# Attention denominators: three of eight weight blocks summed by accumulating transfers into DRAM, one of eight on TensorE, four on VectorE

## The chip, the cores and the metric

The kernel runs on one core of one Trainium2 chip. The metric is device time in microseconds (us). The kernel before takes 4078.07 us, the median of 2 runs (4075.41 to 4080.73).

## The reference, cut to what matters

Two graph layers over 4096 nodes with 512 features in 4 heads, all in float32. Layer 0 runs attention twice (an encoder and a decoder with the same weights), layer 1 once. For every attention the unnormalised weight of source node m for target node n is a masked function of two scalars, and the output row is divided by the sum of its weights.

```python
# layer 0: scores = sigmoid(f1[n] + f2[m]), masked by the adjacency, softmax over m
sig = jax.nn.sigmoid(f1[:, :, None] + f2[:, None, :])
local_att = _masked_softmax(local_pattern[None] * sig, lmask)
Xa = jnp.einsum('hij,hjd->hid', att, Xw)          # encoder
Y = jnp.einsum('hij,hjd->hid', att, Yh)           # decoder, the same att
# layer 1: leaky ReLU of e_s[n] + e_n[m], masked, softmax over m
attn = jax.nn.softmax(logits, axis=-1)
out = jnp.einsum('hnm,hmo->hno', attn, feats)
```

The denominator of the softmax is the sum of the weights over m. How that sum is formed is what the change alters.

## The kernel before, in words

The three attentions are called "enc", "dec" and "gat" and are all built by one function, `attention` (L204). It loops over two blocks of 2048 target nodes (`tb`) and four heads (`h`); one such pass is called a pair here, and each attention has 8 pairs. Inside a pair, `j` (L241) runs over the 32 blocks of 128 source nodes. Block j works on one tile `e` of 128 x 2048 float32 (1024 KB): 128 source nodes on the partitions, 2048 targets along the row.

For each j the weights are computed into `e` and then used:

- enc (and three blocks of four in dec): ScalarE runs a tanh (L288) and an exp (L289) on the whole tile, VectorE multiplies by the 0/1 mask (L290).
- gat: ScalarE runs one Relu (L439), VectorE one fused add-and-multiply (L440).
- TensorE multiplies the tile with the value block of the head, four products of 512 columns, into four PSUM tiles `po` that accumulate over all j (L255).
- In enc, each block with j % 4 = 3 is also stored to DRAM (`ekeep`, L253, from the SP queue); dec loads those again instead of computing them (L249). Masks are loaded from the SP queue for two blocks at a time (L245).

Denominators are formed in enc and gat only (`sums` is set); dec uses the reciprocals of enc again. Before the change, `e` of the blocks with j % 8 in (1, 4, 6) is summed over its partitions by a product with a matrix of ones on TensorE (`add_to_den`, L234 to L237, four products of 32 output rows, into the PSUM tile `den`). The other five of eight are added up on VectorE into a tile `acc` (the first by a copy, L262, the others L265). At the end of a pair `acc` goes through the ones product too; `den` is copied (L275), sent through DRAM in three small transfers from the POOL queue (L277, L279, L282), spread over all partitions as `rb` (L283) and multiplied onto the outputs on GpSimd (L296 in enc, L449 in gat). In gat a Relu (L450), transposes on TensorE (L453) and an addition (L455) follow.

What sets the order of work around the change: the tiles `e` come from a pool of three buffers (`epool`, bufs=3), so ScalarE can begin a tile only when everything that reads the third tile before it is done: the products, the addition or ones product, and any store of it. `po` comes from a pool of seven PSUM banks, `den` from one. Each engine runs its instructions in the order that the scheduler wrote; transfers are issued by SP or POOL in the order of those queues, and a queue that waits holds everything behind it. The rows of scores for a later pair (`rowb`, L224) also go through POOL.

Of the kernel before, what the change touches and what calls it, by code (L numbers as in the profile page):

```python
# [26 lines left out]
FP = mybir.dt.float32  # L27
U8 = mybir.dt.uint8
AF = mybir.ActivationFunctionType
ALU = mybir.AluOpType  # L30
# [4 lines left out]
N, F, H, D, P = 4096, 512, 4, 128, 128  # L35
# [5 lines left out]
TB = 2048  # L41
NTB = N // TB
# [20 lines left out]
def kernel(ctx, tc, x, adjT, w0, w0T, v0, wencT, wdecT, vecs, w1, w1T, a1, out):  # L63
    nc = tc.nc
    consts = ctx.enter_context(tc.tile_pool(name="consts", bufs=1))
    big = ctx.enter_context(tc.tile_pool(name="big", bufs=1))
    dram = ctx.enter_context(tc.tile_pool(name="dram", bufs=1, space=DRAM))
# [34 lines left out]
    rows = [dram.tile([H, IB], FP, name=f"rows{i}") for i in range(NIB)]  # L102
    dens = [[dram.tile([SB, IB], FP, name=f"dens{h}_{t}") for t in range(NTB)] for h in range(H)]
    rinvs = [[dram.tile([1, TB], FP, name=f"rinvs{h}_{t}") for t in range(NTB)] for h in range(H)]

    ekeep = [[[dram.tile([P, TB], FP, name=f"ekeep{h}_{t}_{k}") for k in range(NJ // 4)] for t in range(NTB)]
             for h in range(H)]
# [6 lines left out]
    def everywhere(d, row=0):  # L114

        n = d.shape[-1]
        return bass.AP(tensor=d.tensor, offset=d.offset + row * n, ap=[[0, P], [1, n]])
# [86 lines left out]
    def attention(what, weights, finish, rowprep=None, evacuate=None, sums=None, kept=None):  # L204

        with tc.tile_pool(name=f"{what}_a", bufs=2 if evacuate else 3) as apool, tc.tile_pool(name=f"{what}_r", bufs=2) as rpool, \
                tc.tile_pool(name=f"{what}_e", bufs=3) as epool, tc.tile_pool(name=f"{what}_s", bufs=1) as spool, \
                tc.tile_pool(name=f"{what}_po", bufs=7, space=PSUM) as po_pool, \
                tc.tile_pool(name=f"{what}_ps", bufs=1, space=PSUM) as ps_pool:
            for tb in range(NTB):  # L220
                for h in range(H):
                    rowb = rpool.tile([P, TB], FP, name="rowb")
                    for s in range(SB):
                        nc.gpsimd.dma_start(rowb[:, s * IB:(s + 1) * IB], everywhere(rows[tb * SB + s], h))  # L224
                    if rowprep is not None:
                        rowprep(rowb, h)
                    rb = spool.tile([P, TB], FP, name="rb")
                    if sums is None:
                        nc.gpsimd.dma_start(rb, everywhere(rinvs[h][tb]))
                    else:  # L230
                        acc = spool.tile([P, TB], FP, name="acc")
                        den = ps_pool.tile([P, IB], FP, name="den")

                    def add_to_den(t, start, stop):  # L234
                        for s in range(SB):
                            nc.tensor.matmul(den[s * 32:(s + 1) * 32, :], ones, t[:, s * IB:(s + 1) * IB],  # L236
                                             start=start, stop=stop)  # L237

                    po = [po_pool.tile([P, IB], FP, name="po") for _ in range(SB)]
                    first = True  # L240
                    for j in range(NJ):  # L241
                        e = epool.tile([P, TB], FP, name="e")
                        if j % AG == 0:
                            a2 = apool.tile([P, AG, TB], U8, name="a2")
                            nc.sync.dma_start(a2, masks[tb][j // MG][(j % MG) * P:(j % MG + AG) * P, :]  # L245
                                              .rearrange("(t p) i -> p t i", p=P))
                        store = j % 4 == 3 and kept is not None
                        if store and kept == "read":
                            nc.sync.dma_start(e, ekeep[h][tb][j // 4])  # L249
                        else:  # L250
                            weights(e, rowb, a2[:, j % AG, :], j, h)
                            if store:
                                nc.sync.dma_start(ekeep[h][tb][j // 4], e)  # L253
                        for s in range(SB):
                            nc.tensor.matmul(po[s], V[j // C][:, j % C, h * D:(h + 1) * D], e[:, s * IB:(s + 1) * IB],  # L255
                                             start=(j == 0), stop=(j == NJ - 1))
                        if sums is None:
                            continue
                        if j % 8 in (1, 4, 6):
                            add_to_den(e, j == 1, False)  # L260
                        elif first:
                            nc.vector.tensor_copy(acc, e)  # L262
                            first = False
                        else:
                            nc.vector.tensor_add(acc, acc, e)  # L265
                    if evacuate is None:
                        outs = [X[tb * SB + s][:, h, :] for s in range(SB)]
                        for s in range(SB):
                            nc.scalar.copy(outs[s], po[s])  # L269
                    else:  # L270
                        outs = evacuate(spool, h, po)
                    if sums is not None:
                        add_to_den(acc, False, True)
                        dsb = spool.tile([P, IB], FP, name="dsb")
                        nc.scalar.copy(dsb, den)  # L275

                        nc.gpsimd.dma_start(dens[h][tb], dsb[0:P:32, :])  # L277
                        dcol = spool.tile([P, TB // P], FP, name="dcol")
                        nc.gpsimd.dma_start(dcol, dens[h][tb].rearrange("s (q k) -> (s q) k", k=TB // P))  # L279
                        nc.vector.tensor_scalar(dcol, dcol, sums[0], None, sums[1])  # L280
                        nc.vector.reciprocal(dcol, dcol)  # L281
                        nc.gpsimd.dma_start(rinvs[h][tb].rearrange("o (p k) -> (o p) k", k=TB // P), dcol)  # L282
                        nc.gpsimd.dma_start(rb, everywhere(rinvs[h][tb]))  # L283
                    for s in range(SB):
                        finish(h, tb * SB + s, outs[s], rb[:, s * IB:(s + 1) * IB], spool, po_pool)
# [12 lines left out]


    attention("enc", tanh_weights, finish_enc, sums=(TINY, ALU.max), kept="write")  # L300


# [43 lines left out]
    def finish_dec(h, ib, xs, rb, spool, po_pool):  # L346
# [5 lines left out]
        nc.vector.scalar_tensor_tensor(xs, xs, 0.0, ex, ALU.max, ALU.add)  # L352

    attention("dec", tanh_weights, finish_dec, kept="read")


# [91 lines left out]
    def finish_gat(h, ib, o, rb, spool, po_pool):  # L448
# [7 lines left out]
        if h == H - 1:  # L456
            nc.sync.dma_start(out[ib * IB:(ib + 1) * IB, :].rearrange("(c p) f -> p c f", p=P), X[ib])

    attention("gat", gat_weights, finish_gat, rowprep_gat, evac_gat, sums=(N * TINY, ALU.add))


# [39 lines left out]
```

## Time and profile before

| | |
|---|---|
| median of 2 runs | 4078.07 us |
| profiled execution, its own time | 4079.67 us |
| span of that execution | 4077.9 us |
| granted TensorE clock, mean over the span | 0.951 |
| PE / DVE / ACT / POOL busy | 3588.5 / 2812.2 / 2531.6 / 228.4 us |
| HBM read / written | 407.53 / 92.67 MB |

The span is the time from the first to the last instruction of one profiled execution. PE is TensorE's matmuls, PEld its weight loads, DVE is VectorE, ACT is ScalarE, POOL is GpSimd; "SPq" and "POOLq" in a line is a transfer being issued there. In the list of groups a line reads: source line, engine, operation, output<-inputs, shapes, count | busy us, mean ns of one instruction | idle time of the engine just before those instructions and what ended it. A float32 product of 512 columns is two matmul instructions in the trace, so one `add_to_den` shows as 8. In a timeline the columns are start in us, duration in us, engine, line, operation, count, and in brackets the idle time before it and its releaser. The line numbers are those of the kernel before; the change shifts those below it by two to thirteen.

### The profile page before, as it was taken

The page shows a single profiled execution, that of the slowest core. Times are in us where ns is not written, and L with a number is a line of the kernel's source. Part 1 is how long each engine was busy: PE and PEld are TensorE (multiplying, and loading weights), DVE is VectorE, ACT ScalarE, POOL GpSimd, SP SyncE. Part 2 cuts the span into 40 slices and gives each one's busy share as a digit, 9 for nine tenths or more (in the row PEclk, how much of TensorE's full clock was granted, in tenths as well). Part 3 has the DMA queues.
Part 4 walks back from the last instruction along what each step waited for, and adds up shares of the span by engine and source line. Part 5 has one row for each costly group of instructions (what it writes and reads, how often), then busy time and mean ns, then how long its engine had stood idle before and what let it go on. Part 6 is the DMA issues. An engine that isn't in the chain of part 4 may idle for free. (4 is left out here: it accounts for less than half of the span.)

```text
span 4077.9 us, 27394 instructions
## 1 busy us (share of the span) xinstructions
PE 3588.5 (88%) x10312; PEld 1554.0 (38%) x10312; DVE 2812.2 (69%) x1965; ACT 2531.6 (62%) x1607; POOL 228.4 (6%) x280
## 2 busy tenths in 40 slices
PE   0979999999999789999999999799879889988987
PEld 0733333333333354333334344355333333333432
DVE  2468888898889654555454556832779779778876
ACT  0178988998889248777778874211445445445543
POOL 0000000000000000000000000000000000000000
PEclk9989999999999899999999999889889889989988
DMA  9834434443433124344443442200222122222112
GB/s 166 88 119 145 135 134 138 136 141 128 144 129 119 42 57 146 143 165 158 151 160 141 153 154 78 77 7 1 79 71 78 62 73 78 104 73 83 62 62 88
DMA packets 159253, 434.89 MB, mean 107 GB/s; under 512 B 12176, under 2 KB 12688, under 8 KB 139536
## 3 DMA queue, kind: packets, MB, share of 16 engines
q1 hardware_dynamic: 137408, 365.07, 25.4%
q0 software_dynamic: 20992, 67.51, 8.6%
q8 instruction: 81, 1.33, 0.1%
q10 hardware_dynamic: 720, 0.55, 0.0%
q14 instruction: 52, 0.43, 0.0%
HBM read 407.53 MB, written 92.67 MB: 123 GB/s over the span
## 5 line engine op out<-in xcount | busy, mean ns | idle before, releaser
L255 PE MATMUL po<-e,V 128*128 128x512 f32 x6144 | 2770.2, 606 | 155.1 <-DVE e L290 113.4
L255 PEld LDWEIGHTS po<-e,V 128*128 128x128 f32 x6144 | 1157.3, 193 | 1765.4 <-issue 1481.6
L290 DVE TENSOR_TENSOR e<-e,a 128x2048 f32<-128x2048 f32 x448 | 1023.9, 2289 | 569.6 <-ACT e L289 565.6
L288 ACT ACTIVATE e<-rowb,jcol 128x2048 f32<-128x2048 f32 x448 | 893.0, 1995 | 259.6 <-PE po L255 176.7
L289 ACT ACTIVATE e<-e 128x2048 f32<-128x2048 f32 x448 | 854.1, 1910 | 12.7
L439 ACT ACTIVATE e<-rowb,nq,jcol 128x2048 f32<-128x2048 f32 x256 | 535.9, 2094 | 463.5 <-PE po L255 255.7
L265 DVE TENSOR_TENSOR acc<-acc,e 128x2048 f32<-128x2048 f32 x304 | 696.6, 2291 | 10.0
L440 DVE SCALAR_TENSOR_TENSOR e<-e,jcol,a 128x2048 f32<-128x2048 f32 x256 | 599.5, 2347 | 76.7 <-ACT e L439 73.4
L236 PE MATMUL den<-e,ones 128*32 128x512 f32 x1536 | 207.8, 613 | 18.6 <-DVE e L440 13.9
L224 POOL DMA_DIRECT2D rowb<-rows x96 | 51.9, 548 | 2380.0 <-ACT e L288 1332.2
L406 PE MATMUL pv<-w1s,hT 128*128 128x512 f32 x256 | 139.8, 638 | 1.8 <-ACT hT L145 1.8
L453 PE MATMUL po<-ident,og 128*128 128x128 f32 x128 | 35.7, 434 | 120.1 <-ACT og L450 117.3
L308 ACT ACTIVATE re<-z,vec 128x512 f32<-128x512 f32 x64 | 44.0, 688 | 146.8 <-DVE ex L307 146.8
L321 PE MATMUL z<-X,wenc 128*128 128x512 f32 x256 | 111.6, 599 | 22.6 <-DVE X L163 22.6
L144 PE MATMUL pt<-ident,hn 128*128 128x128 f32 x256 | 37.4, 295 | 93.8 <-DVE hn L141 93.8
L321 PE MATMUL z<-X,wdec 128*128 128x512 f32 x256 | 110.1, 592 | 3.1 <-ACT X L269 3.1
L145 ACT ACTIVATE hT<-pt 128x512 f32<-128x512 f32 x64 | 35.2, 595 | 118.5 <-PE pt L144 118.5
L450 ACT ACTIVATE og<-og,vec 128x512 f32<-128x512 f32 x32 | 23.1, 722 | 125.1 <-POOL og L449 125.1
L121 ACT ACTIVATE rstd<-rstd 128x32 f32<-128x32 f32 x2 | 0.5, 229 | 156.4 <-DVE rstd L120 156.4
L236 PEld LDWEIGHTS den<-e,ones 128*32 128x32 f32 x1536 | 30.4, 108 | 165.1 <-issue 140.3
L455 DVE TENSOR_TENSOR X<-X,po 128x512 f32<-128x512 f32 x32 | 22.0, 688 | 102.6 <-PE po L453 102.6
L408 ACT COPY V<-pv 128x512 f32<-128x512 f32 x32 | 18.8, 586 | 112.4 <-PE pv L406 112.4
(117 smaller groups left out, 1511.7 us busy)
## 6 DMA issues: line engine op xcount, KB each, us to landing
a<-mask SPq DMA_DIRECT2D x384, 512.0 KB
ekeep<-e SPq DMA_DIRECT2D x64, 1024.0 KB
e<-ekeep SPq DMA_DIRECT2D x64, 1024.0 KB
rowb<-rows POOLq DMA_DIRECT2D x96, 256.0 KB, 6.7
rb<-rinvs POOLq DMA_DIRECT2D x24, 1024.0 KB, 5.3
mask<-in_adjT POOLq DMA_DIRECT2D x8, 2048.0 KB, 111.8
X<-in_x SPq DMA_DIRECT2D x8, 1024.0 KB
xt<-in_x SPq DMA_DIRECT2D x8, 1024.0 KB
```

What stands on the lines that cost most here:

```text
L224: nc.gpsimd.dma_start(rowb[:, s * IB:(s + 1) * IB], everywhere(rows[tb * SB + s], h))
L236: nc.tensor.matmul(den[s * 32:(s + 1) * 32, :], ones, t[:, s * IB:(s + 1) * IB], start=start, stop=stop)
L255: nc.tensor.matmul(po[s], V[j // C][:, j % C, h * D:(h + 1) * D], e[:, s * IB:(s + 1) * IB], start=(j == 0), stop=(j == NJ - 1))
L265: nc.vector.tensor_add(acc, acc, e)
L288: nc.scalar.activation(e, rowb, AF.Tanh, bias=jcol[:, j, h:h + 1], scale=0.5)
L289: nc.scalar.activation(e, e, AF.Exp, scale=0.5)
L290: nc.vector.tensor_mul(e, e, a)
L308: nc.scalar.activation(re, src, AF.Relu, bias=bias)
L321: nc.tensor.matmul(z, w[:, fb, o * P:(o + 1) * P], X[ib][:, fb, :], start=(fb == 0), stop=(fb == C - 1))
L406: nc.tensor.matmul(pv, lhsT, w1s[:, fb, :], start=(fb == 0), stop=(fb == C - 1))
L439: nc.scalar.activation(e, rowb, AF.Relu, bias=nq[:, j, h:h + 1], scale=jcol[:, j, h:h + 1])
L440: nc.vector.scalar_tensor_tensor(e, e, jcol2[:, j, h:h + 1], a, ALU.add, ALU.mult)
```

## The change

The split of the denominator sum over the 32 blocks of a pair is new in enc and gat; dec is untouched. Blocks with j % 8 = 3 (four of a pair) go through the ones product on TensorE. Blocks with j % 8 in (1, 4, 6) (twelve of a pair) are sent from `e` to DRAM by transfers from the POOL queue: the first two are plain writes into the two tiles `dacc` of the pair, the other ten add to them in the transfer, alternating between the two. Blocks with j % 8 in (0, 2, 5, 7) (sixteen of a pair, one copy and fifteen additions) are added up on VectorE. At the end of the pair both `dacc` tiles are loaded through the SP queue into tiles of the same pool of three, and each goes through the ones product, ahead of `acc`.

```diff
--- before.py
+++ after.py
@@ -102,6 +102,8 @@
     rows = [dram.tile([H, IB], FP, name=f"rows{i}") for i in range(NIB)]
     dens = [[dram.tile([SB, IB], FP, name=f"dens{h}_{t}") for t in range(NTB)] for h in range(H)]
     rinvs = [[dram.tile([1, TB], FP, name=f"rinvs{h}_{t}") for t in range(NTB)] for h in range(H)]
+
+    dacc = [[[dram.tile([P, TB], FP, name=f"dacc{h}_{t}_{k}") for k in range(2)] for t in range(NTB)] for h in range(H)]
 
     ekeep = [[[dram.tile([P, TB], FP, name=f"ekeep{h}_{t}_{k}") for k in range(NJ // 4)] for t in range(NTB)]
              for h in range(H)]
@@ -237,7 +239,7 @@
                                              start=start, stop=stop)
 
                     po = [po_pool.tile([P, IB], FP, name="po") for _ in range(SB)]
-                    first = True
+                    first, moved = True, []
                     for j in range(NJ):
                         e = epool.tile([P, TB], FP, name="e")
                         if j % AG == 0:
@@ -256,8 +258,15 @@
                                              start=(j == 0), stop=(j == NJ - 1))
                         if sums is None:
                             continue
-                        if j % 8 in (1, 4, 6):
-                            add_to_den(e, j == 1, False)
+                        if j % 8 == 3:
+                            add_to_den(e, j == 3, False)
+                        elif j % 8 in (1, 4, 6):
+                            d = dacc[h][tb][len(moved) % 2]
+                            if len(moved) < 2:
+                                nc.gpsimd.dma_start(d, e)
+                            else:
+                                nc.gpsimd.dma_start(d, e, accum_op=ALU.add)
+                            moved.append(j)
                         elif first:
                             nc.vector.tensor_copy(acc, e)
                             first = False
@@ -270,6 +279,10 @@
                     else:
                         outs = evacuate(spool, h, po)
                     if sums is not None:
+                        for d in dacc[h][tb]:
+                            e = epool.tile([P, TB], FP, name="e")
+                            nc.sync.dma_start(e, d)
+                            add_to_den(e, False, False)
                         add_to_den(acc, False, True)
                         dsb = spool.tile([P, IB], FP, name="dsb")
                         nc.scalar.copy(dsb, den)
```

## The prediction

> **What bounds the kernel now.** I read the groups first: which engine has most work, and what each piece costs.
>
> ```profile
> L255 PE MATMUL po<-e,V 128*128 128x512 f32 x6144 | 2770.2, 606 | 155.1 <-DVE e L290 113.4
> L290 DVE TENSOR_TENSOR e<-e,a 128x2048 f32<-128x2048 f32 x448 | 1023.9, 2289 | 569.6 <-ACT e L289 565.6
> L288 ACT ACTIVATE e<-rowb,jcol 128x2048 f32<-128x2048 f32 x448 | 893.0, 1995 | 259.6 <-PE po L255 176.7
> L289 ACT ACTIVATE e<-e 128x2048 f32<-128x2048 f32 x448 | 854.1, 1910 | 12.7
> L439 ACT ACTIVATE e<-rowb,nq,jcol 128x2048 f32<-128x2048 f32 x256 | 535.9, 2094 | 463.5 <-PE po L255 255.7
> L265 DVE TENSOR_TENSOR acc<-acc,e 128x2048 f32<-128x2048 f32 x304 | 696.6, 2291 | 10.0
> L236 PE MATMUL den<-e,ones 128*32 128x512 f32 x1536 | 207.8, 613 | 18.6 <-DVE e L440 13.9
> ```
>
> The ones products are cheap: 1536 instructions are 192 blocks, 207.8 / 192 = 1.08 us each (four products of 32 rows overlap), against 2770.2 / 768 = 3.6 us for the main products of one block. Next, the table of windows, cut by pair, from one issue of L277 to the next. Columns: busy us with counts for PE, PEld, DVE, ACT, POOL, then clock, DMA share, GB/s. First a pair of enc, then of gat:
>
> ```profile
> core 0: us, PE busy (x) PEld busy (x) DVE busy (x) ACT busy (x) POOL busy (x), PEclk, DMA share, GB/s
> 644.88:782.88 138.00, 129.51 (x361) 49.96 (x360) 119.10 (x59) 125.16 (x70) 9.88 (x12) 0.98 0.41 137
> 3311.93:3459.51 147.58, 130.12 (x376) 52.94 (x376) 122.14 (x59) 74.37 (x43) 9.92 (x13) 0.93 0.23 72
> ```
>
> Enc is paced by ScalarE: 125 of 138 us busy, 3.85 us a block in the timeline, where the ready weights then hold TensorE and VectorE. Gat is paced by TensorE: 3.5 us a block plus 1.05 for each ones product, 8 x 3.5 + 3 x 1.05 = 31.2 us per eight blocks, and some 20 us at the pair's end. Dec has no sums.
>
> Then the three buffers of `e`. The timeline of a stored block in enc shows how much time a transfer that reads `e` has:
>
> ```profile
> 418.88 0.33 SPq L253 DMA_DIRECT2D ekeep<-e  x1
> ...
> 423.85 2.00 ACT L288 ACTIVATE e<-rowb,jcol 128x2048 f32<-128x2048 f32 x1 [0.35 <-DMA ekeep<-e]
> ```
>
> The store starts as the mask product ends, lands in 4.97 us, and ScalarE has already waited 0.35 us for it. There is no spare time: whatever holds a tile longer than about 5.3 us stalls ScalarE. What transfers cost (queue 1 of the page, then issues, the last number us to landing):
>
> ```profile
> q1 hardware_dynamic: 137408, 365.07, 25.4%
> rb<-rinvs POOLq DMA_DIRECT2D x24, 1024.0 KB, 5.3
> ```
>
> A POOL transfer of 1024 KB takes 5.3 us from issue to landing. Queue 1 moves 365.07 MB in 25.4% of 4077.9 us, 2.84 us per MB, so one more pass of 1024 KB (1.05 MB) costs the 16 engines 3.0 us.
>
> **What the skill says.** "DMA: Bandwidth & Descriptors", section "Rules for kernel authors", says that an accumulating transfer reads its destination and writes it later, so that the next one on the same bytes must wait for its semaphore; the built instruction order has these waits on POOL. "Collectives: The Full Stack", section "The bandwidth ceiling: the fold count and why AG ≠ RS ≠ AR", says the add itself is free but needs two source reads, so a reduction runs at about half the rate of a copy. No row of this trace has an accumulating transfer, so this is the unknown. "SBUF — State Buffer", section "Who interferes with whom", says a VectorE operation with two SBUF inputs contends with GpSimd reads; the L277 issues take 0.59 us in enc and up to 1.45 in gat, which would fit.
>
> **The change, part by part**, per pair.
>
> Removed and moved on TensorE: before 12 + 1 ones products, now 4 + 2 + 1, so 6 x 1.05 = 6.3 us less. In gat that is on the pacing engine. In enc it is hidden behind ScalarE, except for its waits on ones products: 22.6 us in 880 us (6.4 pairs), 3.5 us a pair, which I credit. VectorE loses 4 of 20 operations, 4 x 2.29 = 9.2 us, hidden: it has 119 of 138 and 122 of 148 us. If it were the bound this would be a gain; it is not.
>
> Added: 2 plain writes, 10 accumulating transfers, 2 loads. Call T the time of an accumulating transfer from issue to landing. A plain one is 5.3 (the `rb` row). With a second read, 5.3 + 3.0 = 8.3 on idle engines. Only the added 3.0 has not been measured beside other traffic; at a DMA share of 0.41 in enc it becomes 3.0 / 0.59 = 5.1, at about 0.2 in gat 3.0 / 0.8 = 3.7. So T = 10.4 in enc and 9.0 in gat. Bounds: 5.3 (the read fully overlapped) and about 16 (three times the added pass and more).
>
> Enc, stalls. ScalarE's start on block j+3 waits for the transfer of j: 3.85 (tanh, exp) + 0.05 + 2.29 (mask) + T after its start on j. Undisturbed, three blocks are 11.55 us. The stall is T − 5.35 = 5.05 us. Moved blocks 1, 4 and 6 of eight chain as 1→4→7; block 6→9 falls exactly into the stall of 7. So two stalls per eight blocks; the first two of a pair are behind plain writes and cost nothing: 6 x 5.05 = 30.3. In the built order of a pair, two moved blocks run their tanh, then the next block's tanh, then their exp: 2 x 2.0 = 4. Less the 3.5: 30.8 us. ScalarE waits in queue order, so the exp and the next tanh stand behind each stall, then VectorE, then TensorE.
>
> Enc, pair end. TensorE takes both loads' ones products before the next pair. Let a be the end of the last exp. Block 30's transfer lands near a + 8, its load (another 5) at a + 13, and the next pair's products begin at a + 15. ScalarE meanwhile idles 3.4 for the last products, then copies `po`, prepares two tiles and waits about 2 us more: 5.6 together, against the 7.5 a pair it now loses there to `acc` (48.3 us in 6.4 pairs). I take 0; if the cover fails, it is the 8 us of gat. Sum: 8 x 30.8 = 246.
>
> Gat. TensorE can have block j+3 no earlier than T + 2.1 + 2.35 = 13.45 after block j. Eight blocks: 13.45 + 13.45 + 7.0 = 33.9 against 31.2 now; without stalls 29.1. Three times +2.7 and once −2.1 is +6.0. Pair end: block 30's transfer lands T − 3.5 after block 31's weights are ready, the load takes 5.3 and two ones products 2.1; TensorE would have been free after 4.65, so it waits T − 0.75 = 8.25. The chain through `rb` to the transposes stays as it is and starts that much later, for TensorE waits in order:
>
> ```profile
> 3459.51 1.45 POOL L277 DMA_DIRECT2D dens<-dsb  x1 [10.51 <-ACT dsb L275]
> ...
> 3475.96 4.80 PE L453 MATMUL po<-ident,og 128*128 128x128 f32 x16 [14.15 <-ACT og L450]
> ```
>
> On POOL the next pair's block 1 write stands between L277 and L279 and its block 4 write behind the four multiplications; both blocks are ready about when their turn comes, 0. On SP two mask loads stand behind the wait for the second `dacc` load; they serve blocks four later, 0. Sum: 8 x 14.25 = 114.
>
> Total against the profiled execution: 4079.67 + 246 + 114 = 4440. Its time stands 1.6 us above the median of the runs, which I neglect.
>
> **Rivals.**
> Cheap accumulation (0.12): the second read hides behind the write, T near 6. Enc: 6 x 0.65 + 0.5 = 4.4 a pair, +35; gat: 4 x −2.1 + 5.25 = −3.15, −25. About 4090: not slower. For it: 59% of the DMA time is free even in enc. Against: each engine must move half as much again. It decides below T = 7.
> Full relief (0.04): T near 5 and the pair ends free too; gat gains 8 x 6.3 = 50 and enc 28, 4000. Against: the load at the pair's end follows a transfer of the block before last, with 4.65 us to cover 10.
> Costly accumulation (0.34): the added pass costs three times a plain one, 9 us, T = 14.3 everywhere. Enc 6 x 8.95 + 0.5 = 54 a pair, +434; gat 13.3 x 3 − 2.1 + 13.55 = 51, +410: 4920. The engines would then be full: 57 us of present traffic (0.41 x 138), 14 passes of 3.0 and 10 of 9 are 189 of 192 us. For it: the page lists the transfers from POOL as software_dynamic, 67.51 MB in 8.6% of the engines' span, 5.2 us per MB against 2.84, and nothing here has run an accumulating one. Above T = 16 DMA itself sets the pace.
>
> **How the numbers follow.** The likeliest case (0.50), T between 8.3 and 12, runs from 4300 (T = 8.3: +146, +75) to 4630 (T = 12 in enc, 11 in gat: +323, +226), with 4440 at my T. The range 4160 to 5080 leaves out nearly all of the two cases below (0.12 together) and a quarter of the costly one (0.08). 2% is about what a measurement of this kernel can tell from no change: 3996 to 4160. Faster: half of full relief, 0.02. Same: the rest of it and two thirds of cheap accumulation, 0.10. Slower: 0.88.
>
> **What would show it.** Right: ScalarE's and TensorE's waits in enc name `dacc` transfers; landing of the accumulating transfers 8 to 12 us; ones products of L238 waiting for the loads some 8 us a pair; enc pairs near 169 us, gat near 162; a DMA share above 0.7 in enc; dec unchanged. Wrong: landing near 5 us and pairs of 138, or a DMA share at 0.9 and pairs near 200; or POOL issues that take several us each, which I put at 0.55.

## The result and the profile after

The changed kernel takes 4569.38 us (median of 2 runs, 4567.38 to 4571.38) against 4078.07: 1.1205 times as long, 95% interval 1.1157 to 1.1253. Forecast were 4440 us and a range of 4160 to 5080. The profiled execution took 4567.38 us, its span is 4565.6, the mean granted TensorE clock 0.909 (before 0.951).

The groups of the page, for the lines shown of before (L301 was L288, L274 was L265, L257 was L255, L238 was L236; L268 is new, the accumulating transfer):

```profile
L257 PE MATMUL po<-e,V 128*128 128x512 f32 x6144 | 2873.3, 625 | 467.4 <-DVE e L303 305.7
...
L301 ACT ACTIVATE e<-rowb,jcol 128x2048 f32<-128x2048 f32 x448 | 891.8, 1996 | 510.8 <-DMA dacc<-e 267.6
...
L274 DVE TENSOR_TENSOR acc<-acc,e 128x2048 f32<-128x2048 f32 x240 | 549.8, 2291 | 7.2
L268 POOL DMA_DIRECT2D dacc<-e x160 | 138.0, 863 | 1748.6 <-DVE e L303 839.8
L238 PE MATMUL den<-e,ones 128*32 128x512 f32 x768 | 116.8, 683 | 137.2 <-DMA e<-dacc 137.2
```

VectorE and the ones products did what the change says: 240 additions instead of 304, 768 ones instructions instead of 1536. But ScalarE's tanh now stands idle for 510.8 us instead of 259.6, most of it for `dacc` transfers, TensorE's main products for 467.4 instead of 155.1, and the ones products wait 137.2 us for the loads, 8.6 us in each of 16 pairs.

The windows, cut by pair as before (from one issue of the first small transfer to the next), first enc, then gat:

```profile
core 0: us, PE busy (x) PEld busy (x) DVE busy (x) ACT busy (x) POOL busy (x), PEclk, DMA share, GB/s
756.30:931.82 175.52, 134.23 (x314) 52.89 (x313) 110.06 (x55) 125.41 (x70) 19.16 (x25) 0.88 0.71 190
3847.40:4022.40 175.00, 134.87 (x328) 55.51 (x328) 113.60 (x57) 73.74 (x43) 19.10 (x24) 0.85 0.63 168
```

In enc ScalarE has the same 125.4 us of work in a pair that is 37.5 us longer. Over seven pairs the mean is 174.7 us in enc (before 138.1) and 173.4 in gat (before 148.1): 8 x 36.6 + 8 x 25.3 = 495 us, against 491 us between the medians; so enc and gat hold the whole difference. The forecast was 246 us in enc (292 measured) and 114 in gat (202). The transfers, from the page:

```profile
q0 software_dynamic: 48640, 268.85, 29.6%
...
dacc<-e POOLq DMA_DIRECT2D x192, 1024.0 KB, 7.9
...
rb<-rinvs POOLq DMA_DIRECT2D x24, 1024.0 KB, 6.3
```

Median landing is 7.9 us; the accumulating ones alone run from 7.5 to 12.7, the plain first writes come down to 4.2, and `rb` has gone from 5.3 to 6.3.

**Enc, balanced wait by wait.** ScalarE's waits in one pair (581 to 757 us) sum to 49.0 us, against 11.9 in the pair of before. They split as: 24.4 for accumulating transfers (eight waits); 5.9 for TensorE's products, before 0.8; ones products and stores in the pair 0, before 3.7; start of the pair 8.1, before 7.4; end of the pair 10.6, before 0. The last two are worth a look. The start, in the timelines, before and then after:

```profile
664.43 0.69 DVE L297 BATCH_NORM_STATS2 st_att<-X 128x6 f32<-128x512 f32 x1 [0.54 <-POOL X L296]
665.04 2.27 DVE L265 TENSOR_TENSOR acc<-acc,e 128x2048 f32<-128x2048 f32 x1
...
667.40 2.00 ACT L288 ACTIVATE e<-rowb,jcol 128x2048 f32<-128x2048 f32 x1 [6.00 <-DVE acc L265]
```

```profile
773.26 0.54 POOL L296 DMA_DIRECT2D rb<-rinvs  x1 [5.79 <-issue]
773.79 0.54 POOL L266 DMA_DIRECT2D dacc<-e  x1
...
783.54 3.90 ACT L301 ACTIVATE e<-rowb,jcol 128x2048 f32<-128x2048 f32 x2 [8.09 <-DMA dacc<-e]
```

Before, the four statistics of the previous pair stand in VectorE's queue and wait for `rb`; an addition stands behind them, and ScalarE waits 6.0 us for that. After, ScalarE's 8.1 us go to block 4's first write, which POOL issues right behind `rb` and which then lands in 9.6 us, not in 4.2. It looks like a new wait of 8 us, but the old one lies under it: the first and the ninth experiment below show a wait of about that length without such a write. The end, ScalarE's timeline before and then after:

```profile
776.37 2.00 ACT L288 ACTIVATE e<-rowb,jcol 128x2048 f32<-128x2048 f32 x1 [0.28 <-PE den L236]
778.28 1.54 ACT L269 COPY X<-po 128x512 f32<-128x512 f32 x3
```

```profile
736.50 0.59 ACT L278 COPY X<-po 128x512 f32<-128x512 f32 x1 [3.54 <-PE po L257]
...
740.11 2.00 ACT L301 ACTIVATE e<-rowb,jcol 128x2048 f32<-128x2048 f32 x1 [0.44 <-PE den L238]
745.81 2.00 ACT L301 ACTIVATE e<-rowb,jcol 128x2048 f32<-128x2048 f32 x1 [3.70 <-DMA ekeep<-e]
...
753.53 2.00 ACT L301 ACTIVATE e<-rowb,jcol 128x2048 f32<-128x2048 f32 x1 [2.12 <-PE den L238]
```

Before, the next pair's tanh ran ahead of the copies of `po`, so ScalarE never waited for the last products. After, the two loads take the next two tiles of the pool of three. The next pair's first tile is then the one of block 31, and that is still being multiplied and stored; the copies come first in ScalarE's queue and wait, then the tanh wait for the store and for the loads' ones products.

**Gat, in TensorE's timeline after:**

```profile
3882.71 1.07 PE L238 MATMUL den<-e,ones 128*32 128x512 f32 x8
3883.71 28.02 PE L257 MATMUL po<-e,V 128*128 128x512 f32 x64
3911.66 1.07 PE L238 MATMUL den<-e,ones 128*32 128x512 f32 x8
3916.60 16.46 PE L257 MATMUL po<-e,V 128*128 128x512 f32 x32 [3.88 <-DVE e L453]
...
3948.95 1.06 PE L238 MATMUL den<-e,ones 128*32 128x512 f32 x8
...
4017.58 1.94 PE L238 MATMUL den<-e,ones 128*32 128x512 f32 x8 [6.26 <-DMA e<-dacc]
```

Here one ones product marks every eight blocks. The first eight, behind plain writes, take 3911.66 - 3882.71 = 28.95 us (forecast 29.1), the next eight 37.3 (forecast 33.9). Before, with three ones products in eight blocks, it was 31.05 us from block 4's to block 12's:

```profile
3499.28 1.06 PE L236 MATMUL den<-e,ones 128*32 128x512 f32 x8
...
3530.33 1.07 PE L236 MATMUL den<-e,ones 128*32 128x512 f32 x8
```

The pair's end grew too. From TensorE's last main product of a gat pair to the first of the next the mean over seven pairs is 35.0 us, before 24.4. The sum of the two, three times some 6, once -2.2, and 10.6, is 26 us, near the 25.3 of the pair lengths.

### The profile page after: what moved, and what is told of

Same layout as the page of the kernel before. It is cut to its first block, busy times and chain, and to the rows that moved or that the text cites. A ratio compares the mean times of both kernels' runs of the same rounds, so it can differ in the third digit from the quotient of the medians.

```text
span 4565.6 us, 26391 instructions
## 1 busy us (share of the span) xinstructions
PE 3629.8 (80%) x9544; PEld 1584.3 (35%) x9544; DVE 2673.2 (59%) x1901; ACT 2527.8 (55%) x1607; POOL 380.2 (8%) x472
## 5 line engine op out<-in xcount | busy, mean ns | idle before, releaser
L257 PE MATMUL po<-e,V 128*128 128x512 f32 x6144 | 2873.3, 625 | 467.4 <-DVE e L303 305.7
L257 PEld LDWEIGHTS po<-e,V 128*128 128x128 f32 x6144 | 1198.3, 200 | 2146.2 <-issue 1420.1
L301 ACT ACTIVATE e<-rowb,jcol 128x2048 f32<-128x2048 f32 x448 | 891.8, 1996 | 510.8 <-DMA dacc<-e 267.6
L274 DVE TENSOR_TENSOR acc<-acc,e 128x2048 f32<-128x2048 f32 x240 | 549.8, 2291 | 7.2
L268 POOL DMA_DIRECT2D dacc<-e x160 | 138.0, 863 | 1748.6 <-DVE e L303 839.8
L238 PE MATMUL den<-e,ones 128*32 128x512 f32 x768 | 116.8, 683 | 137.2 <-DMA e<-dacc 137.2
L466 PE MATMUL po<-ident,og 128*128 128x128 f32 x128 | 35.7, 435 | 138.1 <-ACT og L463 135.4
L238 PEld LDWEIGHTS den<-e,ones 128*32 128x32 f32 x768 | 15.8, 113 | 214.3 <-DMA e<-dacc 160.5
```

What stands on the lines that cost most here:

```text
L268: nc.gpsimd.dma_start(d, e, accum_op=ALU.add)
L301: nc.scalar.activation(e, rowb, AF.Tanh, bias=jcol[:, j, h:h + 1], scale=0.5)
```

## The experiments

Times are medians; ratios, with 95% intervals, are to the kernel before on the same chip (4078.5 to 4083.6 us). Pair lengths are means over seven pairs.

**No moved sums at all.** The twelve moved blocks are summed nowhere, and there are no loads: the pure relief.

```diff
-                            d = dacc[h][tb][len(moved) % 2]
...
-                            moved.append(j)
+                            pass
...
-                        for d in dacc[h][tb]:
-                            e = epool.tile([P, TB], FP, name="e")
-                            nc.sync.dma_start(e, d)
-                            add_to_den(e, False, False)
```

> The twelve moved blocks are summed nowhere and nothing is loaded at the pair's end (their part of the denominators is left out); the rest of the split is as in the changed kernel. Theory (the loss comes from the transfers: tiles of e held by them, and the loads at the pair's end): only the relief is left, 8 x 1.05 us per gat pair = 67 and 3.5 per enc pair = 28, about 3985 us. Rival (the new split and the order of instructions that comes with it cost by themselves): 4080 or more.

3984.62 us, 0.9768 (0.9753 to 0.9782); pairs 133.8 in enc, 141.4 in gat. The relief is worth 4.3 and 6.7 us a pair. The total came out as expected, the parts less so: 3.5 and 8.4 were expected, since here eight ones products of a gat pair go. ScalarE still waits at the start of a pair, with no transfer of `e` but the stores; the products that it waits for begin only when VectorE is through the four statistics:

```profile
659.49 2.00 ACT L292 ACTIVATE e<-rowb,jcol 128x2048 f32<-128x2048 f32 x1 [7.07 <-PE po L257]
```

**All twelve writes plain.** Ten blocks' sums are overwritten, thus left out.

```diff
-    nc.gpsimd.dma_start(d, e, accum_op=ALU.add)
+    nc.gpsimd.dma_start(d, e)
```

> The ten accumulating transfers of a pair become plain writes of the same size to the same place (ten block sums are left out); waits, loads and ones products stay. Theory (it is how long a transfer holds its tile): 7.9 us from issue to landing become about 5.7, most stalls inside a pair go, 17 us an enc pair and 11 a gat pair, about 4340 us; what remains is the pair's start and end. Rival (holding time doesn't matter, traffic from POOL and the ends do): 4540 or more.

4258.43 us, 1.0435 (1.0418 to 1.0453); pairs 155.4 and 153.4; the twelve writes of a pair have a median landing of 4.6 us. So accumulating alone costs 19.3 us a pair in enc and 20.0 in gat, more than the 17 and 11 expected. What is left, 21.6 and 12.0 us a pair above the run without transfers, belongs to the writes, the two loads and the loads' ones products together. In gat the writes themselves are little of it: eight blocks take 29.7 us, against 28.95 without transfers, but from the last main product of a pair to the first of the next TensorE takes 35.6 us, against 25.2. These 10.4 of the 12.0 us lie at the pair's end, where a ones product waits for the second load:

```profile
3772.31 1.93 PE L238 MATMUL den<-e,ones 128*32 128x512 f32 x8 [9.40 <-DMA e<-dacc]
```

**Four tiles of e in enc** (and two mask tiles in enc and dec, to make room).

```diff
-        with tc.tile_pool(name=f"{what}_a", bufs=2 if evacuate else 3) as apool, ...
+        with tc.tile_pool(name=f"{what}_a", bufs=2) as apool, ...
-                tc.tile_pool(name=f"{what}_e", bufs=3) as epool, ...
+                tc.tile_pool(name=f"{what}_e", bufs=4 if what == "enc" else 3) as epool, ...
```

> The changed kernel with four buffers of e in enc instead of three, paid for by two buffers of masks instead of three in enc and dec. Theory (the third buffer is what is late): a fourth gives 3.85 us more, 15.4 against 6.2 + 7.9, so the stalls in enc go, some 28 us a pair, about 4345 us; gat as before. Rival (DMA bandwidth or the POOL queue sets the pace in enc, so buffers don't help): 4520 or more. If two mask buffers are too few, dec gets longer, which would show there.

4466.56 us, 1.0948 (1.0932 to 1.0965): a miss. The enc pair fell only to 161.1 us, DMA share 0.77. In the pair from 716 us on, ScalarE's waits for `dacc` within the pair shrank to 0.5 to 3.0 us each, 17.4 in all, but at the pair's end one of 9.5 us remained, for the transfer of block 30, which landed in 15.2. The transfers had themselves grown longer: over all enc pairs the accumulating ones land in 9.0 us (median), in the changed kernel in 7.8.

**The accumulating transfers without the loads.** Their part of the sums is left out.

```diff
-                        for d in dacc[h][tb]:
-                            e = epool.tile([P, TB], FP, name="e")
-                            nc.sync.dma_start(e, d)
-                            add_to_den(e, False, False)
```

> The accumulating transfers stay, but their two tiles are not loaded at the pair's end and not put through the ones product (their part of the denominators is left out). Theory: the end of a pair costs 8 to 11 us in both stages, 16 pairs, about 4410 us. Rival (in enc it is covered by ScalarE, as the prediction had it): about 4490 us.

4495.08 us, 1.1015 (1.0998 to 1.1033): the time that the rival gave, but not for its reason. Pairs are 170.6 and 169.0, so the loads are worth 4.1 us a pair in enc, where the rival had none, and 4.5 in gat, where it had 8 to 11. Without them the next pair's tiles are those of blocks 29 and 30, and in enc ScalarE waits 5.5 us there for block 30's transfer instead.

**First writes from SP instead of POOL.**

```diff
-    nc.gpsimd.dma_start(d, e)
+    nc.sync.dma_start(d, e)
```

> The changed kernel, but the two plain first writes of a pair are issued from SP instead of POOL, so that they don't stand behind the chain that brings rb. Theory (in enc, block 7 of the next pair waits 8.1 us because block 4's write stands on POOL behind the transfer for rb): those 8 us go, in enc only, 8 x 8 = 64, about 4505 us; in gat POOL already waits for VectorE there, 0. Rival (the wait only moves on to block 6's transfer, which stands behind the four multiplications): 4550 or more.

4616.54 us, 1.1298 (1.128 to 1.1315): the rival, and slower than the changed kernel. Block 7 no longer waits, but block 6's accumulating transfer now stands on POOL behind the four multiplications, which wait for `rb` (some 9 us from its issue, with the SP write and mask loads beside it), and block 9 waits in ScalarE:

```profile
632.50 2.00 ACT L301 ACTIVATE e<-rowb,jcol 128x2048 f32<-128x2048 f32 x1 [14.45 <-DMA dacc<-e]
```

**Control: the kernel before with four tiles of e in enc.** Same edit of the two pools.

> Control for the fourth buffer: the kernel before, with four buffers of e and two of masks in enc, two of masks in dec. Theory: the kernel before hardly waits for a buffer in enc (3.3 us for stores in 6.4 pairs), so within 1%, 4040 to 4110 us. Rival (the buffers help by themselves, whatever the denominators do): 3 us a pair or more, below 4040.

4023.72 us, 0.9852 (0.9838 to 0.9865): the rival. This is the fastest full version found, and beats both kernels. The fourth tile covers the wait behind the statistics at the start of a pair (6.0 us before, absent here; 3.2 us for a store remain, and the enc pair is 130.7). Against this control the change with four tiles costs 443 us; with three it costs 491.

**Four tiles and first writes from SP.** Both edits above.

> Both mends of the changed kernel together: four buffers of e in enc and the two first writes from SP. Theory: enc pairs go from 161 us (four buffers alone) to about 152, gat stays near 173, 4400 us. Both remain slower than before, because gat alone has lost 25 us a pair. Rival (with the queue free and a fourth buffer nothing is left in enc): enc pairs near 138, below 4300.

4494.83 us, 1.1003 (1.0987 to 1.1018): a miss; enc pairs 164.0, no gain over four tiles alone.

**The kernel before with one ones product of three moved to VectorE in gat.**

```diff
-    if j % 8 in (1, 4, 6):
+    if j % 8 in ((1, 4) if what == "gat" else (1, 4, 6)):
```

> The kernel before with two of eight blocks on the ones product in gat (1 and 4) instead of three, block 6 added up on VectorE; enc as before. No transfers. Theory (TensorE paces gat, 1.05 us for a ones product; VectorE has 122 of 148 us): TensorE loses 4.2 us a pair, VectorE gets 9.2 and is at 131, so up to 4 us a pair are gained, about 4050 us. Rival (VectorE becomes the pace in the blocks where two additions follow each other): 4080 or more.

4075.38 us, 0.998 (0.9971 to 0.999): a miss, near the rival; gat pairs 147.4, only 0.7 less for four ones products less (4.2 us). 2.3 us were lost again at the pair's end: from the main products of one pair to those of the next TensorE takes 26.7 us, before 24.4, and there the ones product of `acc` waits 2.46 us for the last addition on VectorE, which now has block 30 as well.

**Moved blocks only from j = 8 on.** Nothing is left out.

```diff
-    if j % 8 == 3:
-        add_to_den(e, j == 3, False)
+    if j % 8 == 3 or (j % 8 in (1, 4, 6) and not j >= 8):
+        add_to_den(e, j == 1, False)
```

> Moved blocks only for j of 8 and more: the three early ones of a pair (1, 4, 6) are summed by the ones product as before the change, so that no first write stands on the POOL queue beside the three transfers of the denominators, with 2 plain and 7 accumulating transfers a pair instead of 2 and 10. Theory (block 7's wait of 8.1 us a pair comes from that queue, and each removed accumulating transfer takes its stall of some 3 us with it): enc pairs some 19 us shorter (near 156), gat pairs some 5 shorter (near 168), about 4380. Rival (the start of the pair is not the cause; the wait moves to blocks 12 and 15): 4500 or more.

4541.5 us, 1.1129 (1.1112 to 1.1146): the rival. Pairs 173.0 and 171.5. Up to here I read the 8.1 us at the start of a pair as a cost of the first writes. With no first write near it, ScalarE waits there all the same:

```profile
782.37 2.00 ACT L301 ACTIVATE e<-rowb,jcol 128x2048 f32<-128x2048 f32 x1 [3.51 <-DVE acc L274]
...
790.96 2.01 ACT L301 ACTIVATE e<-rowb,jcol 128x2048 f32<-128x2048 f32 x1 [4.66 <-PE den L238]
```

The four statistics again stand in VectorE's queue until `rb` has come, and these waits follow from that: the first for an addition behind them, the second for the ones product of block 6, whose mask product stands behind them too. The changed kernel has no ones product of block 6, so this run alone would not show the point; the 7.1 us of the run without transfers, which are there for the same statistics, bear it out. Two waits lie over each other, and taking one away leaves the other.

**Moved blocks only for 8 <= j < 24**, six a pair, loads possible long before the pair's end.

```diff
-    if j % 8 == 3:
-        add_to_den(e, j == 3, False)
+    if j % 8 == 3 or (j % 8 in (1, 4, 6) and not 8 <= j < 24):
+        add_to_den(e, j == 1, False)
```

> Moved blocks only for 8 <= j < 24: six a pair, 2 plain and 4 accumulating transfers, the others on the ones product as before the change; both loads can come long before the pair's end. Theory (costs are the queue at the pair's start, one stall for each accumulating transfer, and the loads at the end): enc pairs near 143, gat pairs near 155, about 4170. Rival (the loads, taken in at the pair's end as the program places them, still hold TensorE there, or the first writes stall ScalarE anywhere): 4260 or more.

4368.2 us, 1.0703 (1.0685 to 1.0721): the rival. Pairs 158.4 and 165.9. ScalarE loses 9.9 us at the end of an enc pair, nearly what it loses in the changed kernel, with the copies ahead of the next tanh again, though the last moved block is 22; one ones product still waits 4.9 us for a load. So block 30's late landing is not all that sits there; the loads' place in the pool and in the queues has a part, though no run sets its size.

**TensorE's gaps in gat filled** with products of zeros, which add nothing.

```diff
+    zeros = consts.tile([P, 32], FP, name="zeros")
+    nc.gpsimd.memset(zeros, 0.0)
...
+    if what == "gat" and j in (12, 20, 28):
+        for k in range(3):
+            for s in range(SB):
+                nc.tensor.matmul(den[s * 32:(s + 1) * 32, :], zeros,
+                                 V[0][:, s, :], start=False, stop=False)
```

> The changed kernel, and in gat, ahead of the products of blocks 12, 20 and 28, twelve products of a matrix of zeros added to the denominators (adding nothing), which keep TensorE busy for some 3.2 us in which it otherwise waits. Theory (after 3.85 us of idleness TensorE's granted clock falls, and its next 32 matmuls take 16.5 us instead of 14.0): with the gap filled they take 14.0 again, three times 2.5 us in each of eight gat pairs, 60 us, about 4510. Rival (those matmuls are slow for another reason, such as the transfers running beside them): no gain, 4560 or more.

4602.2 us, 1.1288 (1.1266 to 1.131): my theory on the time fell. TensorE's timeline there:

```profile
3950.22 2.76 PE L261 MATMUL den<-V,zeros 128*32 128x512 f32 x24
3956.01 16.92 PE L264 MATMUL po<-e,V 128*128 128x512 f32 x32 [3.03 <-DVE e L460]
...
3988.53 1.06 PE L240 MATMUL den<-e,ones 128*32 128x512 f32 x8
3989.41 2.76 PE L261 MATMUL den<-V,zeros 128*32 128x512 f32 x24
3993.01 10.57 PE L264 MATMUL po<-e,V 128*128 128x512 f32 x24 [0.83 <-DVE e L460]
4005.76 8.83 PE L264 MATMUL po<-e,V 128*128 128x512 f32 x16 [2.19 <-DVE e L460]
```

Where the gap is down to 0.83 us, 24 instructions take 10.57 us, full speed (64 take 28.02 elsewhere); after a gap of 3.0 they do not. Yet from block 12's start to block 20's are still 3993.01 - 3956.01 = 37.0 us, as without the filling (37.25), and after block 20, where the filling did close the gap, it is 37.2: TensorE then waits later. Its clock is a consequence here, not what sets the pace. The pair grew by 5.2 us, most of it at its end: from the first small transfer to the third are 9.2 us instead of 5.9, since block 1's write waits on POOL between them and an addition stands ahead of the reciprocals on VectorE.

**One mask load a pair in gat.** All 32 blocks use what the first load brought, the masks of two blocks, so their weights are not the reference's.

```diff
-    if j % AG == 0:
+    if j % AG == 0 and (what != "gat" or j == 0):
```

> The changed kernel with one mask load a pair in gat instead of sixteen: all 32 blocks of a pair use the first one's mask, so the weights of the others are not the reference's; every instruction of the engines stays. In the changed kernel the transfers of blocks with j % 8 = 1 in gat land after 9.9 to 10.6 us with two mask loads of 512 KB beside them, others after 7.6 to 9.2, and eight blocks take 37.2 us: two transfers on the path, 10.6 and 9.4 us from issue to ScalarE's start, and 17.2 of ScalarE and VectorE. Theory (the mask loads beside them stretch these transfers): all land near 7.6, eight blocks take about 33 us, gat pairs about 13 us less (160), enc and dec unchanged, about 4460. Rival (they are late for a reason of their own, the tile they add to or the order on their queue): landings as before, gat pairs within 3 us of 173.4, 4540 or more.

4506.27 us, 1.1057 (1.1039 to 1.1076): the landing as the theory said, the time between theory and rival. Landing of the ten accumulating transfers of one gat pair, changed kernel first, then this one:

```profile
DMA to landing us min/median/max: 7.6/8.5/10.6
```

```profile
DMA to landing us min/median/max: 7.4/7.6/10.4
```

The nine that have no other load beside them land in 7.4 to 7.7 (the tenth shares with loads at the pair's end). Gat pairs fell to 164.7 us, eight blocks to 34.1. Expected were 160 and 33.

## Why the prediction was right, and where its steps failed

Direction, mechanism and range held: the loss does come from tiles that transfers hold and from the loads at the pair's end, the waits name `dacc` transfers, and the DMA share in enc is 0.71. The sizes held less well. Pairs were to be 169 and 162 us and are 174.7 and 173.4; 360 us were forecast and 491 measured, inside a range that was wide. Gat's part came out at nearly twice the forecast, and that enc's came near owes something to luck, as two errors there point opposite ways. Differences between three kernels and the one before split the change as follows (us a pair; the parts add up by construction):

| part | enc | gat |
|---|---|---|
| relief of TensorE and VectorE | -4.3 | -6.7 |
| twelve plain writes, two loads and their ones products | +21.6 | +12.0 |
| ten of the writes accumulate | +19.3 | +20.0 |
| sum = change | +36.6 | +25.3 |

The accumulating read is only part of the story. The rival of cheap accumulation would have failed even with a landing of 4.6 us (1.0435 with plain writes): it counted 5.25 us for gat's pair end, where the run with plain writes shows 35.6 - 24.4 = 11.2.

**Relief** (6.3 us in gat, 3.5 in enc): near in enc, 4.3. In gat the measured 6.7 is for eight ones products less, the forecast 6.3 for six, since the loads bring two back. So a product less was worth 0.84 us there and not 1.05, and that the two sums agree is chance.

**T.** The step "at a DMA share of 0.41 in enc it becomes 3.0 / 0.59 = 5.1" oversized T in enc: ten transfers of a pair land in 8.8 us on average, not 10.4, and the free floor is 7.5, not 8.3. Against 4.2 for a plain write the floor is 1.8 times as long, near the half rate that the prediction drew on; the accumulation itself adds 3.3. The form was wrong as well: the stretch does not follow the mean share of the stage but what lies beside the single transfer. In the two pairs read transfer by transfer (581 to 757 and 3847 to 4023 us) those of blocks with j % 8 = 1 land in 9.7 to 10.6, in gat with two mask loads of 512 KB beside them, and the others in 7.5 to 9.2, but for block 30 in enc, 12.1 beside a store, a load of `dacc` and the rows for a later pair. The last run shows the cause for gat, where taking the mask loads away took the stretch away. For gat's path T was therefore undersized: two transfers in every eight blocks, 10.6 and 9.4 us from issue to ScalarE's start, against 9.0.

**Enc stalls** (6 x 5.05 = 30.3): measured 24.4, in eight shorter waits instead of six, as T is smaller. **Paired tanh order** (4): ScalarE's waits for products rose by 5.1.

**Enc, pair end ("I take 0; if the cover fails, it is the 8 us of gat")**: this is the step that failed, 10.6 us. It set the new waits "against the 7.5 a pair it now loses there to `acc`". That wait is not at the end but at the start, behind the statistics, and it stayed, now in the name of a `dacc` transfer. I had read the releaser of a summed group of waits without looking where in the pair they lie. With the cover gone the sum is 24.4 + 5.1 + 0.7 + 10.6 - 3.7 = 37.1, against 37.0 from the lengths of these two pairs (174.98 and 138.00); the smaller T hides part of the miss (forecast 30.8). The loads are not the whole of the 10.6: without them ScalarE still waits 5.5 us there for block 30's transfer, and the pair is only 4.1 us shorter.

**POOL and SP order (0)**: near zero in its effect at the start of a pair (8.1 in place of 7.4), though not for the reason given: block 4's write came late, but a wait of that length is there anyway. The run without transfers (7.1 us there) and the one with late moved blocks show it, after I had taken the 8.1 for new. It is zero only in this order: with SP issuing the first writes a wait of 14.45 appeared. **POOL issue (0.55)**: 0.86 us for an accumulating transfer, 0.58 for a plain one; the queue had room. The prediction was inclined to lay the slow issues of L277 in gat to VectorE operations with two SBUF inputs. The trace of before says otherwise: each of the six slow ones (0.83 to 1.45 us) lay over the copy of L262, which has one.

**Gat, eight blocks (+2.7)**: measured +6.0, three times a pair. Block 12's start to block 20's is 37.25 us: two transfers (20.0) and 17.25 us of ScalarE and VectorE, against 18.0 and 15.9 in the forecast. So 2.0 of the 3.35 missing are T beside mask loads, and 1.35 are ScalarE and VectorE, most of it an addition that stands ahead of the mask product that the next transfer waits for. Without mask loads the first part goes; the second grew there to 3.0, which is why that run gained 8.7 us a pair and not 13. **Gat, pair end (8.25)**: the right place, somewhat undersized, 10.6. In the pair shown TensorE waits 2.05 + 6.26 us for the loads; the forecast counts 2.1 us of ones products within its 8.25, so its waits proper are 6.15. The chain through `rb` stayed as it was, as forecast: from the first small transfer to the transposes 15.4 us, before 16.5. With the loads gone 29.0 of the 35.0 us between the main products of two pairs remain, against 25.2 in the run without any transfer.

Left open: how much of the 10.6 at enc's pair end is the tiles taken by the loads, how much the order of ScalarE's queue, and how much block 30's late landing. No run moved one of them alone. Four tiles helped the changed kernel in enc by 13.6 us a pair but the kernel before by 7.4, so one tile more takes away only some 6 us of what the change costs; the longer landings that came with it may have eaten the rest.

## What to carry to other kernels

A transfer that reads a tile of a small rotating pool is paid in the time for which it holds the tile: compare its landing with the slack of that pool (in enc some 5.3 us), transfer by transfer and with what else moves at that moment. In gat, writes that landed in 4.6 us cost next to nothing inside a pair, accumulating ones of 7.5 us and more cost 20 us. Loads at the end of a pass, into tiles of the same pool, cost time of their own, which no slack inside the pass covers. Before a wait is set against another one, find where in the pass each lies; when two lie over each other, taking one away gains little.

## What the runs showed of the hardware

An accumulating transfer of 1024 KB into DRAM landed in 7.5 us at best, a plain one in 4.2; issuing it took POOL 0.86 us instead of 0.58. In gat, with two loads of 512 KB beside it, it landed in 10.5 or 10.6 us; with these loads taken away, in 7.4 to 7.7.

POOL's issue of a transfer did not end while VectorE ran its copy of 128 x 2048 float32 (1.22 us). Before the change six issues in gat fell on such a copy; they took 0.83 to 1.45 us, and each ended 0.09 to 0.10 us after the copy. One issue at 3459.51 took 1.45 us and ended at 3460.96; the copy had run from 3459.64 to 3460.86. Beside VectorE's operations with two inputs an issue stays short: in the changed kernel, at 3848.00, 0.59 us inside a mask product of 2.35 us.

TensorE was slow after some short gaps, and what that cost was mostly the same. In gat of the changed kernel 24 instructions took 12.26 us instead of 10.57 after gaps of 3.84, 3.88 and 2.34 us; in the filled run, after a gap of 2.19 us, 16 took 8.83 instead of 7.13. Each time 1.7 us were lost. In the pair shown above 32 took 16.46 us instead of 14.0 after a gap of 3.88, which is more; and 24 took the usual 10.57 after a gap of 3.40. After the gap of 0.83 us in the filled run 24 took 10.57. The Trainium skill, "TensorE: Matmul & The Clock Gate", section "What's actually happening", describes a clock that is halved after an idle window of about 3.4 us, a window that runs freely, until a busy one has passed. An estimate from that page, 3.4 us at half speed, is a loss of 1.7 us, which agrees. That the length of a gap does not settle whether it costs anything fits a window that runs freely. But gaps of 2.2 to 2.4 us are shorter than the page's window, and no run here shows why they were enough.
